# A feed-forward's first rows in their own memory, a shared expert's output by pairs of tiles, and sums spread before a transposition

## The chip, the cores and the metric

The kernel runs on one core of a Trainium2 chip. A core has five engines with their own instruction streams: TensorE (PE in the profile; PEld is its weight load), VectorE (DVE), ScalarE (ACT), GpSimd (POOL) and SyncE (SP). POOL and SP issue most DMAs. The metric is the device time in microseconds (us) of one execution. The kernel before takes 1120.72 us (median of three runs, 1116.92 to 1121.18).

## The reference

x is 4 x 512 rows of 512 numbers, 2048 rows in all, 16 tiles of 128. Four layers follow each other, each on a layer-normalized x, each added to x with a gain:

```
x = x + tanh(g_xattn[0]) * L0_xattn(layernorm(x), itok, ctx)    # 4 gated experts, chosen by token id, weights = ctx
x = x + tanh(g_ffn[0])   * L0_ffn(layernorm(x), wg, wu, wd)     # gated, 512 -> 2048 -> 512, block floating point
x = x + tanh(g_xattn[1]) * L1_xattn(layernorm(x), ctx, ctx)     # softmax attention, 8 heads, times gamma
x = x + tanh(g_ffn[1])   * L1_ffn(layernorm(x), ...)            # 64 experts, 6 per row, plus a shared expert
```

In the feed-forward of layer 0 activations and weights are rounded in blocks of 32 to a shared exponent and a short mantissa. The shared expert of the last layer is

```
shared = silu(x @ ws_gate) * (x @ ws_up) @ ws_down              # 512 -> 192 -> 512
```

## The kernel before

The stages run one after the other and pass x through memory.

**Routed layer (to about 228 us).** Rows are sorted by their token's expert into 19 tiles. The loop `for i in range(-2, NS)` is a software pipeline written out by hand: per step it turns tile i's activations (sT) and tile i+2's rows (hT) with TensorE transposes that ACT copies out of PSUM, multiplies them with the context, squashes and gates, and scatters y_sb with an accumulating indirect DMA (L495, POOL) into `x_rows`. Beside it, `some_weights(us)` hands DVE and ACT a stretch of the rounding of the feed-forward's weights; `turn_weights` transposes what is rounded. A `while` loop behind it finishes the weights. The engines' order here is the order of the program text.

**Feed-forward (to 480).** Every row tile j is loaded from x_rows (`load`, L670, SP), then: sums for the layer norm (`sums_of`: two ACT passes with accumulation, L150), factors for a group of tiles (`factors_from`: a chain of small DVE operations with three Newton steps, L156 to L163), scaling (`normal`, ACT), rounding (`block_scales`, `block_round`, DVE; ACT spreads the scale as mx_wide, L694), transposes (`turned_rows`, h_ps L731, hT L733), gate and up products in four chunks (`gate_up`, L758), silu (ACT) and the product (`times_up`, DVE, L769), rounding of the hidden row, transposes, `down`, and an accumulating store to x_rows. Tile j+1 is prepared inside step j. Nine buffers `xt` hold the rows, in memory that the routed layer used until its end. Here and in the attention PE, ACT and DVE follow the text; SP and POOL are ordered by a scheduler.

**Attention (to about 750).** One loop over n = 4 j + i. Step (j, i) computes the scores of a pair of heads' quarter (at_s, L632), their maxima (low, DVE L637) and exponentials (p, ACT L646), and transposes the p of two steps earlier (p_ps L958, pT L959; two PSUM buffers of tag "t", which h_ps of `turned_row` shares). Beside it goes work for earlier tiles: `values` (at_o, L991), `over_sums` (the reciprocal of the sums, DVE), `spread_sums` (over_ps, L972: 16 small matmuls that lay the reciprocals over the columns; ACT scales them into r, L977), `weighted` (r times at_o, DVE L999), `attended`, `row`, `turned_row` (h_ps L1034, hT L1039), `first_layer` (router and, for the six tiles AT_ONCE, the shared expert's first products, L1048), `hidden_at_once`, `groups_of`, `experts_of` (top-k on DVE) and `noted` (scatters, POOL). over_ps, at_o, at_ps and first_ps share two PSUM buffers of tag "m".

**Experts and shared output (to the end).** For each of 64 experts rows are gathered (POOL), turned, multiplied with weights streamed by SP, and scattered with accumulation, even experts into `out`, odd ones into `more_rows`; the last one goes into `out`. Then, for each of 16 tiles, `turn_shared` transposes the tile's 192 hidden numbers in two halves of 96 (L1441), ACT copies them out, two matmuls of 96 rows with `shared_dn` give sh_y (L1451), DVE adds the tile of `more_rows` (rest, L1453), and POOL issues an accumulating store into `out` (L1454).

## Time and profile before

| what | us |
|---|---|
| median of the runs | 1120.72 |
| the profiled execution | 1129.35 |
| its span | 1127.6 |
| PE busy | 989.6 (88%) |
| DVE busy | 747.5 (66%) |
| ACT busy | 586.6 (52%) |
| POOL busy | 387.6 (34%) |

Rows of the profile read: start, duration, engine, line of the kernel, operation, output<-inputs, shapes, count; in brackets the engine's idle time just before and what ended it. A row of the busy time by stretches gives a stretch, its length, and the busy time of PE, PEld, DVE, ACT and POOL with instruction counts, then the granted TensorE clock, the busy share of the DMA engines and GB/s. PE's starts are recorded, its ends modelled.

### The profile page before, as it was taken

Reading aid. Unit: us, or ns where it says so; the run is one execution under the profiler, and the core shown is the slowest. Engines: PE = TensorE matmul, PEld = TensorE weight load, DVE = VectorE, ACT = ScalarE, POOL = GpSimd, SP = SyncE. Lnnn points to the kernel's source line nnn. Section 1 sums busy time; section 2 is a strip of 40 time slices with the busy share of each in tenths; the row PEclk is TensorE's granted clock in tenths of the full one; section 3 lists DMA queues with packets and bytes.
Section 4 is the critical chain, followed back from the end, with each engine's and each line's share of the span. In section 5 each row is a group of like instructions: output and inputs, shape, how many; then the busy total and the mean of one; then the engine's idle time right before and its main releaser. Section 6 shows DMA issues by size and latency. Waiting matters only on the chain.

```text
span 1127.6 us, 14846 instructions
## 1 busy us (share of the span) xinstructions
PE 989.6 (88%) x4630; PEld 506.9 (45%) x4652; DVE 747.5 (66%) x1877; ACT 586.6 (52%) x1151; POOL 387.6 (34%) x526
## 2 busy tenths in 40 slices
PE   4689999736989898899999989987999999999996
PEld 3345554312444444354454544544444444444442
DVE  6899999958999999848888887864222222222222
ACT  4878886546767668586666766641112111111221
POOL 4123322200000000011554545555455555555434
PEclk9699999857999999999999999997999999999998
DMA  7846655330222121193121221015999999999569
GB/s 255 309 122 142 147 112 141 49 120 27 57 47 38 19 24 24 19 304 110 60 67 50 68 69 41 30 41 190 295 342 325 310 308 303 304 308 316 155 171 162
DMA packets 81438, 168.68 MB, mean 150 GB/s; under 512 B 14637, under 2 KB 15677, under 8 KB 81296
## 3 DMA queue, kind: packets, MB, share of 16 engines
q1 hardware_dynamic: 57440, 128.06, 33.7%
q0 software_dynamic: 23200, 39.08, 18.6%
q8 instruction: 38, 0.62, 0.2%
q10 hardware_dynamic: 720, 0.59, 0.2%
q14 instruction: 40, 0.33, 0.1%
HBM read 133.76 MB, written 44.20 MB: 158 GB/s over the span
## 4 chain that ended last, share of the span: by engine, by line
PE 40%; DVE 9%; ACT 4%; issue 2%; POOL 2%; DMA 0%; POOLq 0%; DVEq 0%; ACTq 0%
PE gu_ps L1335 15%; PE e_y L1357 5%; PE at_o L991 4%; PE e_y L1419 3%; DVE low L637 3%; ACT p L646 2%; PE g_ps L1325 2%; PE first_ps L1048 2%; PE at_s L632 2%; PE at_s L1075 2%; ACT pT L959 1%; PE p_ps L958 1%; POOL out_dram L1454 1%; PE sh_y L1451 1%; PE over_ps L972 1%
## 5 line engine op out<-in xcount | busy, mean ns | idle before, releaser
L1335 PE MATMUL gu_ps<-e_gu,gT 128*96 128x384 f32 x512 | 175.7, 486 | 0.0
L1340 DVE SCALAR_TENSOR_TENSOR a<-s,xg,gu_ps 96x192 f32<-96x192 f32 x64 | 26.2, 409 | 146.5 <-ACT s L1337 146.5
L1337 ACT ACTIVATE s<-gu_ps 96x192 f32<-96x192 f32 x64 | 20.9, 327 | 177.7 <-PE gu_ps L1335 177.6
L123 POOL DMA_INDIRECT taken<-token_no,to_i x96 | 95.6, 996 | 37.8 <-issue 23.9
L646 ACT ACTIVATE p<-at_s,low 128x512 f32<-128x512 f32 x128 | 87.8, 700 | 38.4 <-DVE low L637 22.3
L1335 PEld LDWEIGHTS gu_ps<-e_gu,gT 128*96 128x96 f32 x512 | 78.5, 163 | 61.8 <-issue 61.6
L1311 POOL DMA_INDIRECT xg<-h_rows,idx x64 | 63.7, 996 | 99.4 <-DVE a L1340 67.6
L785 POOL DMA_DIRECT2D x_rows<-y_sb x15 | 12.8, 856 | 239.0 <-ACT y_sb L784 176.1
L637 DVE TENSOR_REDUCE low<-at_s 128x2 f32<-128x1024 f32 x64 | 77.7, 1216 | 17.8 <-PE at_s L632 17.8
L495 POOL DMA_INDIRECT x_rows<-y_sb,to_row x19 | 38.3, 2016 | 142.3 <-ACT y_sb L494 142.3
L758 PEld LDWEIGHTS <-hT 128*128 128x128 bf16 x512 | 51.3, 102 | 72.5 <-issue 19.2
L478 PE MATMUL l_mm<-cT,sT 128*128 x152 | 73.7, 630 | 10.5 <-ACT sT L465 10.5
L959 ACT COPY pT<-p_ps 128x512 f32<-128x512 f32 x128 | 69.4, 604 | 25.2 <-PE p_ps L958 22.7
L478 PE MATMUL l_mm<-cT,hT 128*128 x152 | 71.6, 615 | 9.2 <-ACT hT L465 9.2
L758 PE MATMUL gu<-wgT,hT 128*128 128x512 bf16 x246 | 69.6, 400 | 9.5 <-DVE inter L769 7.0
L958 PEld LDWEIGHTS p_ps<-ident,p 128*128 128x128 f32 x512 | 54.8, 141 | 48.1 <-ACT pT L959 24.7
L632 PE MATMUL at_s<-c_tile,q 64*128 64x512 f32 x256 | 72.0, 640 | 4.9 <-ACT p L646 4.9
L1327 DVE COPY gT<-g_ps 128x384 f32<-128x384 f32 x64 | 35.5, 557 | 61.4 <-PE g_ps L1325 58.9
L776 PE MATMUL y<-wdT,iT 128*128 128x512 bf16 x250 | 61.6, 391 | 11.3 <-ACT iT L751 11.2
L958 PE MATMUL p_ps<-ident,p 128*128 128x128 f32 x512 | 70.2, 280 | 0.4 <-ACT pT L959 0.2
L758 PE MATMUL gu<-wuT,hT 128*128 128x512 bf16 x250 | 67.7, 393 | 0.2
L1357 PE MATMUL e_y<-e_dn,eaT 128*96 128x512 f32 x128 | 65.5, 593 | 0.1
(260 smaller groups left out, 2005.2 us busy)
## 6 DMA issues: line engine op xcount, KB each, us to landing
e_gu<-in_L_ffn_w_gate_dram SPq DMA_DIRECT2D x64, 384.0 KB
e_gu<-in_L_ffn_w_up_dram SPq DMA_DIRECT2D x64, 384.0 KB
e_dn<-in_L_ffn_w_down_dram SPq DMA_DIRECT2D x32, 768.0 KB
w_src<-in_L_ffn_w_gate_dram SPq DMA_DIRECT2D x8, 512.0 KB
c_sb<-in_ctx_dram SPq DMA_DIRECT2D x4, 1024.0 KB
w_src<-in_L_ffn_w_up_dram SPq DMA_DIRECT2D x8, 512.0 KB
more_rows<-zeros SPq DMA_DIRECT2D x16, 256.0 KB
w_src<-in_L_ffn_w_down_dram SPq DMA_DIRECT2D x8, 512.0 KB
```

Source lines behind the costliest of these rows:

```text
L123: ins = nc.gpsimd.indirect_dma_start(out=table[:, :], out_offset=bass.IndirectOffsetOnAxis(ap=to, axis=0), in_=what, in_offset=None)
L478: nc.tensor.matmul(ps.unsqueeze(1), aT[:, k, :], cT[:, bass.ds(at + k, 1), :], start=k == 0, stop=k == KC - 1)
L632: nc.tensor.matmul(s[:, h, :], t["q"][rows, bass.ts(i, P)], t["c"][rows, :], start=True, stop=True)
L637: nc.vector.tensor_reduce(low, tiles[j]["s", i], AX.X, ALU.max, negate=True)
L646: nc.scalar.activation(p[:, h, :], s[:, h, :], AF.Exp, bias=low[:, h : h + 1], accum_out=t["sums"][:, i, h : h + 1])
L758: nc.tensor.matmul(ps[:, i, :], hT[:, k, :], wT[:, k, bass.ts(c, 512)], start=k == 0, stop=k == KC - 1)
L776: nc.tensor.matmul(stages[j]["y"], iT[:, c, :], wdT[:, c, :], start=c == 0, stop=c == FI // P - 1)
L958: nc.tensor.transpose(ps[:, k, :], p[:, h, bass.ts(k, P)], ident)
L959: nc.scalar.copy(tiles[j]["pT"][h][:, :, bass.ts(i, P)], ps)
L1311: gathered_by[e] = nc.gpsimd.indirect_dma_start(out=g[:, :], out_offset=None, in_=h_rows[:, :], in_offset=bass.IndirectOffsetOnAxis(ap=idx ...
L1335: nc.tensor.matmul(ps, gT[:, k, :], gu[:, :, k, :], start=k == 0, stop=k == KC - 1)
L1357: nc.tensor.matmul(y, aT, dn, start=True, stop=False)
```

## The change

Three parts. (1) A pool `ffn_rows` of four buffers is opened before the routed layer, in memory of its own; tiles 0 to 3 (and later 9 to 12) of the feed-forward use it, the others five buffers in the old place. Their loads are issued inside the routed layer, ahead of the `while` loop. One round of `some_weights` moves from the end of step NS-2 to behind the sT transposes of step NS-1. The layer norm of tiles 0 to 3 is taken on DVE (`factors_of`: bn_stats and bn_aggr, tile 0 alone, 1 to 3 together) instead of by ACT's passes, and the order before the feed-forward's loop is rewritten so that tile 1 is normalized and rounded, and tile 2 normalized, there. (2) `shared_dn` is laid out as three blocks of 128 rows, in four DMAs, with 64 rows of it at both halves of the middle block; two tiles' 384 hidden numbers are turned in three transposes; each tile's output is one matmul of 128 rows and one of 64. (3) In the attention `spread_sums` is placed ahead of `turned_row`, and `hidden_at_once` ahead of `groups_of`.

```diff
+    rows_pool = tc.tile_pool(name="ffn_rows", bufs=4, side="right")
+    ffn_rows = rows_pool.__enter__()
+    later_rows = [{} for _ in range(NT)]
+
+    def load(j):
+        pool, n = (ffn_rows, 4) if j % 9 < 4 else (fp, 5)
+        xt = pool.tile([P, D], F32, name="xt", bufs=n)
+        nc.sync.dma_start(xt, x_rows[bass.ts(j, P), :])
+        later_rows[j]["x"] = xt
...
             if i >= 0:
                 turned(i, "s", "sT")
+            if i == NS - 1:
+                some_weights(3.6)
...
-            some_weights(3.6)
+            if i != NS - 2:
+                some_weights(3.6)
             factors_from(i + 4)
+        for j in range(4):
+            load(j)
         while rounded or sources or begun:
...
-        groups = [[0], [1, 2, 3], [4, 5, 6, 7], [8, 9, 10, 11], [12, 13, 14, 15]]
+        groups = [[4, 5, 6, 7], [8, 9, 10, 11], [12, 13, 14, 15]]
...
+        def factors_of(g):
+            mv = few.tile([P, len(g), 2], F32, name="ln_mv", tag=f"ln_mv{len(g)}", bufs=1)
+            for i, j in enumerate(g):
+                st = few.tile([P, 6], F32, name="ln_st", bufs=1)
+                nc.vector.bn_stats(st, stages[j]["x"])
+                nc.vector.bn_aggr(mv[:, i, :], st)
+            a = few.tile([P, len(g)], F32, name="ln_a", tag=f"ln_a{len(g)}")
+            nc.vector.tensor_scalar(a, mv[:, :, 1], EPS, None, ALU.add)
+            y = newton(a, small=few)
+            shift = few.tile([P, len(g)], F32, name="ln_shift", tag=f"ln_shift{len(g)}")
+            nc.vector.scalar_tensor_tensor(shift, mv[:, :, 0], -1.0, y, ALU.mult, ALU.mult)
+            for i, j in enumerate(g):
+                stages[j]["stats"] = y[:, i : i + 1], shift[:, i : i + 1]
...
-        for j in range(8):
+        for j in range(4, 8):
             load(j)
-        sums_of(0)
-        factors_from(0)
+        factors_of([0])
         normal(0)
-        sums_of(1)
         block_scales(0, "h", D)
         block_round(0, "h", D)
-        sums_of(2)
         turned_rows(0)
+        for j in range(4, 7):
+            sums_of(j)
+        factors_of([1, 2, 3])
+        normal(1)
         gate_up(0, 0)
         gate_up(0, 1)
-        sums_of(3)
+        block_scales(1, "h", D)
+        block_round(1, "h", D)
         silu(0, 0)
-        factors_from(1)
         silu(0, 1)
-        normal(1)
-        for j in range(4, 7):
-            sums_of(j)
+        normal(2)
...
-    shared_dn = moe.tile([FH, 2, D], F32, name="shared_dn")
+    shared_dn = moe.tile([P, 3, D], F32, name="shared_dn")
...
-        nc.sync.dma_start(shared_dn, ws_down.rearrange("(c p) d -> p c d", p=FH))
+        FL = P // 2
+        for p, n, c, first in ((0, P, 0, 0), (0, FL, 1, P), (FL, FL, 1, 0), (0, P, 2, FL)):
+            nc.sync.dma_start(shared_dn[bass.ds(p, n), c, :], ws_down[bass.ds(first, n), :])
...
                 do(over_sums, j - 1)
+                do(hidden_at_once, j - 3)
                 do(groups_of, j - 3)
                 do(noted, j - 4, range(3))
-                do(hidden_at_once, j - 3)
...
             elif i == 1:
+                do(spread_sums, j - 1)
                 do(turned_row, j - 2)
-                do(spread_sums, j - 1)
...
-        def turn_shared(j):
-            ps = ps_t.tile([FH, 2, P], F32, name="a_ps", tag="t")
-            for c in range(2):
-                nc.tensor.transpose(ps[:, c, :], shared_a[:, j, bass.ts(c, FH)], ident)
-            aT = xp.tile([FH, 2, P], F32, name="aT")
+        def turn_shared(a):
+            ps = ps_t.tile([P, 3, P], F32, name="a_ps", tag="t")
+            two = shared_a[:, a : a + 2, :].rearrange("p j f -> p (j f)")
+            for c in range(3):
+                nc.tensor.transpose(ps[:, c, :], two[:, bass.ts(c, P)], ident)
+            aT = xp.tile([P, 3, P], F32, name="aT")
             nc.scalar.copy(aT, ps)
             return aT
...
-            for c in range(2):
-                nc.tensor.matmul(y, this[:, c, :], shared_dn[:, c, :], start=c == 0, stop=c == 1)
+            for i, y in enumerate(ys):
+                nc.tensor.matmul(y, this[:, 2 * i, :], shared_dn[:, 2 * i, :], start=True, stop=False)
+            for i, y in enumerate(ys):
+                half = bass.ts(i, P // 2)
+                nc.tensor.matmul(y, this[half, 1, :], shared_dn[half, 1, :], start=False, stop=True)
```

Inside the feed-forward's loop, step 0 no longer normalizes tile 2 or rounds tile 1, as both are done ahead of it.

More of the change, by code (lines that the diff above doesn't have):

```diff
@@ L665, in flamingo_kernel @@
     ):
-        stages = [{} for _ in range(NT)]
-        def load(j):
-            xt = fp.tile([P, D], F32, name="xt", bufs=9)
-            nc.sync.dma_start(xt, x_rows[bass.ts(j, P), :])
-            stages[j]["x"] = xt
+        stages = later_rows
         def part_of(j, what):
@@ L797, in factors_from @@
         def factors_from(j):
-            if j < NT and group_of[j][0] == j:
+            if j in group_of and group_of[j][0] == j:
                 g = group_of[j]
@@ L839, in flamingo_kernel @@
             silu(j, 2)
-            if j + 2 < NT:
+            if 0 < j < NT - 2:
                 normal(j + 2)
@@ L843, in flamingo_kernel @@
                 block_scales(j, ("a", 0), FI // 2)
-            else:
+            elif j:
                 block_scales(j + 1, "h", D)
@@ L850, in flamingo_kernel @@
                 block_round(j, ("a", 0), FI // 2)
-            else:
+            elif j:
                 block_round(j + 1, "h", D)
@@ L906, in flamingo_kernel @@
         add_rows(NT - 1)
+    rows_pool.__exit__(None, None, None)
     mx_pool.__exit__(None, None, None)
@@ L1446, in flamingo_kernel @@
         aT = turn_shared(0)
-        for j in range(NT):
-            y = ps_m.tile([P, D], F32, name="sh_y", tag="m")
-            this, aT = aT, turn_shared(j + 1) if j + 1 < NT else None
-            for c in range(2):
-                nc.tensor.matmul(y, this[:, c, :], shared_dn[:, c, :], start=c == 0, stop=c == 1)
-            o = rest[j // 3][:, j % 3, :]
-            nc.vector.scalar_tensor_tensor(o, y, half_f1, o, ALU.mult, ALU.add)
-            nc.gpsimd.dma_start(out[bass.ts(j, P), :], o, accum_op=ALU.add)
+        for a in range(0, NT, 2):
+            this, aT = aT, turn_shared(a + 2) if a + 2 < NT else None
+            ys = [ps_m.tile([P, D], F32, name="sh_y", tag="m") for _ in range(2)]
+            for i, y in enumerate(ys):
[3 more added lines that the diff above has]
+                nc.tensor.matmul(y, this[half, 1, :], shared_dn[half, 1, :], start=False, stop=True)
+            for i, y in enumerate(ys):
+                j = a + i
+                o = rest[j // 3][:, j % 3, :]
+                nc.vector.scalar_tensor_tensor(o, y, half_f1, o, ALU.mult, ALU.add)
+                nc.gpsimd.dma_start(out[bass.ts(j, P), :], o, accum_op=ALU.add)
 _INS = ['x', 'itok_BxS_13_99985', 'ctx_2048', 'g_xattn', 'g_ffn', 'L0_ffn_w_gate', 'L0_ffn_w_up', 'L0_ffn_w_down',
```

## The prediction

> **What bounds the kernel now.** I read the busy time by stretches first, to see the stages: TensorE is busy 287.5 of 289 us in the experts, 219 of 240 in the attention, but 10.7 of 29 where the feed-forward begins.

> ```profile
> 231.00:260.00 29.00, 10.70 (x41) 4.45 (x40) 12.08 (x47) 17.80 (x40) 0.00 (x0) 0.62 0.32 103
> 260.00:480.00 220.00, 189.88 (x1042) 92.00 (x1060) 204.71 (x325) 151.18 (x227) 12.84 (x15) 0.96 0.19 31
> 510.00:750.00 240.00, 219.47 (x1316) 118.87 (x1316) 195.55 (x747) 159.76 (x388) 117.34 (x270) 0.99 0.18 57
> 796.00:1085.00 289.00, 287.54 (x1122) 137.85 (x1122) 76.93 (x195) 56.15 (x131) 147.75 (x121) 1.00 0.95 287
> ```

> After the length stand the busy us of PE, PEld, DVE, ACT and POOL, the granted clock, DMA share and GB/s. From 260 to 480 DVE is the full engine, so what the head of that stage saves passes on.

> Second, the timelines at that head. DVE rounds weights without a gap until 230.06; nothing ready stands behind it.

> ```profile
> 228.09 0.84 SPq L586 DMA_DIRECT2D c_tile<-in_ctx_dram  x2
> 229.37 0.69 DVE L280 TENSOR_TENSOR w_q<-w_q,mx_wide 128x1024 bf16<-128x1024 bf16 x1
> 231.29 2.70 SPq L670 DMA_DIRECT2D xt<-x_rows  x6
> 234.35 0.72 ACT L150 ACTIVATE waste<-xt 128x512 f32<-128x512 f32 x1 [2.51 <-DMA xt<-x_rows]
> 236.04 0.17 DVE L156 TENSOR_SCALAR ln_mean<-ln_sums 128x2 f32<-128x2 f32 x1 [5.98 <-ACT waste L150]
> 243.36 0.58 PE L731 MATMUL h_ps<-ident_bf,mx_c 128*128 128x128 bf16 x4 [12.20 <-DVE mx_c L716]
> 259.15 0.43 DVE L716 TENSOR_TENSOR mx_c<-mx_c,mx_wide 128x512 bf16<-128x512 bf16 x1 [4.34 <-ACT mx_wide L694]
> 259.63 0.61 PE L731 MATMUL h_ps<-ident_bf,mx_c 128*128 128x128 bf16 x4 [5.03 <-DVE mx_c L716]
> 260.92 1.89 PE L758 MATMUL gu<-wgT,hT 128*128 128x512 bf16 x4 [0.68 <-ACT hT L733]
> ```

> The row loads start when the weights' last reader (PE, 231.16) frees the memory, the sums wait for them, TensorE stands still for 12.2 us, and again for 5.0 us because ACT does six passes of sums (252.39 to 257.33) ahead of tile 1's mx_wide.

> Third, the waits in the attention, then its timelines: thirteen times TensorE waits before h_ps, because h_ps needs the PSUM buffer that ACT's first pT copy frees; over_ps, ready, stands behind it.

> ```profile
> PE h_ps L1034 <- ACT pT L959: 9.3, 13, 1.2
> 643.16 0.66 PE L1034 MATMUL h_ps<-ident,hw 128*128 128x128 f32 x4 [0.81 <-ACT pT L959]
> 643.75 1.09 PE L972 MATMUL over_ps<-ident,over 128*64 128x128 f32 x16
> 644.67 3.60 PE L991 MATMUL at_o<-pT,cT 128*64 128x512 f32 x16
> 650.27 0.69 DVE L999 TENSOR_TENSOR r<-at_o,r 128x512 f32<-128x512 f32 x1 [1.88 <-PE p_ps L958]
> ```

> Last, the end of the run, by stretches: the DMA share, not TensorE, is what stays full.

> ```profile
> 1098.49 0.95 POOL L1454 DMA_DIRECT2D out_dram<-rest  x1 [6.34 <-DMA out_dram<-e_o,idx]
> 1102.00:1104.00 2.00, 2.00 (x8) 0.98 (x7) 0.75 (x1) 0.37 (x1) 2.00 (x5) 1.00 1.01 123
> 1110.00:1112.00 2.00, 2.00 (x7) 0.92 (x6) 0.75 (x1) 0.37 (x1) 0.92 (x2) 1.00 1.12 202
> 1118.00:1120.00 2.00, 0.00 (x0) 0.00 (x0) 0.64 (x1) 0.00 (x0) 0.92 (x2) 1.00 1.13 193
> 1120.00:1122.00 2.00, 0.00 (x0) 0.00 (x0) 0.00 (x0) 0.00 (x0) 0.00 (x0) 0.73 1.11 174
> ```

> **First rows (first part).** The moved round of weights puts ACT's sT copy of the last routed tile (214.42) ahead of one mx_wide and one mx_e (1.03 and 1.04 us); its transposes end at 212.31, so sT starts at about 212.6, the last product, y_sb and the scatter come 1.8 us or more earlier. DVE's order does not change: nothing of DVE's lies between the two places. The scatter landed by 228.09 (the first load that waited for it); now by 226.3. The four new loads need only that landing, as their memory was never used: the first lands 3.06 us after issue (231.29 to 234.35), at 229.3, under DVE's weights, which end at 230.06. On SP they go ahead of two c_tile loads, pushed back by 4 x 0.42 us and needed at 473; no weight load is behind them (the last went at 200.45).

> From 230.1: one bn_stats 0.69, one aggregate 0.18, then 13 small operations at 0.19 to 0.20 (the same count as the row's chain from 236.44 on): 3.4 us, to 233.5. The scaling on ACT starts at 233.6 instead of 239.49. mx_c follows at 237.3 (243.14), the first product at 239.1 (245.02). Three more bn_stats and aggregates and one Newton chain (2.7 + 2.5 us) end on DVE at 242.5, beside ACT's six passes for tiles 4 to 6 (4.94 us, from 238.7 to 243.6); the loads of 4 to 7 go at 231.29 as before and cover that. Then normal(1) 0.8, scales and rounding 2.8: mx_c of tile 1 at 247.2 (before 259.58). Now times_up(0,0) is what is late: it stands behind that rounding on DVE, 247.2 instead of 249.32, so the third and fourth gate products start at 247.9 after 2.7 us of idle TensorE and end near 252.0 (254.6 before). The transposes of tile 1 follow at once, its products start at 253.3 to 253.5 instead of 260.92: **-7.4 us**. If DVE's first small tiles lie in memory that the weights' last reader holds, everything starts at 231.2: -6.3. That is one end; the other is -8.0, if the third and fourth products run at the 1.73 us each that they take from 250.99 on, where I allow 4.1 for both after an idle stretch.

> **Sums' spreading (third part).** over_ps (16 matmuls, 0.92 us from start to start) needs `over`, which DVE has at 641.85; TensorE is free at 642.35. It fills the wait, h_ps (0.59) follows, at_o starts earlier by the idle time. What is added is two more changes between whole-array and 64-column matmuls. Four h_ps took 0.59 to the next start where eight p_ps took 0.93 to 1.03: about 0.12 us for a change. So a tile gains its idle minus 0.12: 0.51 where it was 0.63, 0.68 where 0.80. [...]

> Does the gain reach the end? It does where DVE stood idle before weighted (L999), since DVE there waits for the chain through at_o; tiles whose query factors fall in (528.71, 597.81, 669.69) show no idle before it and give nothing, nor does 509.36, behind a late load. Ten are left: 0.58, 0.58, 0.68, 0.64, 0.51, 0.69, 0.68, 0.68, 0.89, 0.51. Tiles at 579.81 and 616.87 are capped by their DVE idle; the one at 720.35 also saves the 0.38 wait of at_o for shared_a, which hidden_at_once ahead of groups_of removes (two operations, 0.6 us, same DVE sum). **-6.4 us**; ends: 0, and -12.2 (all idle before h_ps, 10.7, plus 1.5 for shared_a). I take the count by tile, which is nearest to rows. ACT now does r before hT; the p_ps that needs hT's buffer is 0.5 us later than the copy.

> **Shared output in pairs (second part).** Loading shared_dn takes four DMAs, 768 KB for 384 KB. At 350 GB/s, the rate from 490 to 510, 393 KB more are 1.1 us, in front of the out store and the x_tile load for which DVE waits 5.32 us at 508.53; three more issues at 0.62 us make 1.9 on SP. **+1.1**, ends 0 and +1.9.

> On TensorE a pair of tiles is 2 x 1.94 = 3.88 us now; after it, two whole products (1.72), a pair of 64-row ones (1.03, the row of e_y L1419) and three transposes (0.33): 3.08, 6.4 us less over eight pairs. But the sixteen accumulating stores may begin only at 1098.49, when the last expert's scatter has landed, and then move 4.2 MB at about 203 GB/s with DMA share 1.1 until 1123. At 1106 ten were issued and about four moved; the queue never runs dry, so an earlier issue only lengthens it. **0 us**; ends: -5.8 if issue set the end (last issue 1118.93 to 1113.1), +1.3 if the slow first rate (143 KB/us while POOL issues back to back) lasts for all 14 us of issuing.

> **Sum.** -7.4 - 6.4 + 1.1 + 0 = -12.7 us. The experts in between keep TensorE full, and their weights, landed by 1054 for a last use at 1079, shift with it. Against the profiled execution (1129.35, span 1127.6) that is 1116.6. It was 8.6 us slower than the median of the runs, 1120.72; from the median: **1108.0**.

> **Rivals.** (A) The swap gives nothing: the added changes of matmul shape eat it, or weighted waits for something else. For it: five times DVE waited for ACT's r, not for at_o. Then -6.3 in all: 1114.4. (B) The head moves less, about 3 us: the scaled tile or its scratch waits for freed memory, or ACT's six passes still delay tile 1. Against it: DVE ended at 230.06 with idle to 236. Then 1112.4. (C) The tail follows TensorE after all: 5.8 more, 1102.2; against it the share of 1.1. (D) Slower: r, now ahead of hT on ACT, comes late. Seven r waited up to 2.04 us after hT though over_ps was long done (544.84 against 539.67). hT then ends about 2.1 us after p_ps wants its buffer and TensorE stalls. On all 13 tiles, 2.1 each and no gain, it is 27.3 - 7.4 + 1.1: +21, 1141.7. It decides from 0.92 us lost per tile, (5.6 + 7.4 - 1.1) / 13. Against it: eight r waited not at all, and h_ps now stands between over_ps and at_o. (E) The change does not do what it says: the first rows still land after 231, head -2, others as forecast: 1113.4.

> **How the numbers follow.** Differences under 0.5% (5.6 us) can't be told from none here. Forecast, 1104 to 1112: 0.48. A 0.17, B 0.10, C 0.08, D 0.09, E 0.08. Faster: the forecast, B, C, E (0.74) and, since A lies at -6.3, just past the bound, a third of it: 0.80; same: the rest of A, 0.11; slower: D, 0.09. The range leaves out D and the outer edge of C and A: 1101 to 1117, with the tail's ends and the shared_dn load inside it.

> **What would show it.** Right: xt loads issued before 228 and landed by 230; bn_stats at 230 to 231.3; tile 1's products near 253.4; no wait of h_ps for pT, over_ps in front of it; r's waits no longer; sh_y in steps of about 3.1 us a pair, the DMA share still 1.1 to the end and 23 to 25 us from the first accumulating store to the last byte. Wrong: hT's copy late and p_ps waiting for it; DVE's first bn_stats after 232; a tail shorter by over 2 us.

## The result, and the profile after

The changed kernel takes 1110.02 us (median of seven runs, 1107.29 to 1112.90) against 1120.72 us for the kernel before (median of seven runs, 1116.26 to 1121.32). The ratio is 0.9916, with a 95% interval of 0.9896 to 0.9935: 9.4 us less, between 7.3 and 11.7 (the ratio's distance from 1 times 1120.72). The forecast was 1108.0 and 1101 to 1117. The profiled execution took 1109.52 us (span 1107.7), so unlike the profile of before it lies at its median.

The two profiles are not in step where the change begins: the last gated product of the routed layer starts on DVE at 209.74 before and at 207.69 after. Times below that are called aligned have these 2.05 us added. First the stretches of the changed kernel, as busy us of PE, PEld, DVE, ACT and POOL, granted clock, DMA share and GB/s:

```profile
225.00:254.00 29.00, 14.56 (x63) 6.62 (x64) 19.95 (x58) 14.86 (x31) 0.00 (x0) 0.68 0.31 99
254.00:470.00 216.00, 187.95 (x1053) 91.00 (x1053) 202.71 (x323) 148.69 (x222) 12.85 (x15) 0.97 0.19 31
490.00:730.00 240.00, 230.46 (x1371) 124.98 (x1371) 200.26 (x751) 166.27 (x407) 118.45 (x277) 0.97 0.22 73
776.00:1065.00 289.00, 288.69 (x1125) 138.24 (x1126) 76.05 (x194) 56.28 (x129) 148.81 (x121) 1.00 0.96 287
```

TensorE is busier at the head of the feed-forward (14.6 of 29 us, 10.7 before) and in the attention (230 of 240, 219 before); the experts are as they were. The granted clock in the attention is 0.97 where it was 0.99: this small figure becomes the main finding below.

The head, from the timelines of SP's queue, ACT, POOL, DVE and PE:

```profile
210.48 0.58 ACT L476 COPY sT<-l_ps 128x512 f32<-128x512 f32 x1
221.35 2.06 SPq L191 DMA_DIRECT2D xt<-x_rows  x4
223.98 0.69 DVE L821 BATCH_NORM_STATS2 ln_st<-xt 128x6 f32<-128x512 f32 x1 [2.09 <-DMA xt<-x_rows]
229.61 0.69 DVE L291 TENSOR_TENSOR w_q<-w_q,mx_wide 128x1024 bf16<-128x1024 bf16 x1
231.96 0.82 ACT L170 ACTIVATE h<-xt,ln_shift,ln_y 128x512 f32<-128x512 f32 x1
237.11 1.89 PE L770 MATMUL gu<-wgT,hT 128*128 128x512 bf16 x4 [0.68 <-ACT hT L745]
246.21 1.25 PE L770 MATMUL gu<-wgT,hT 128*128 128x512 bf16 x4 [4.04 <-DVE inter L781]
252.68 1.04 PE L770 MATMUL gu<-wgT,hT 128*128 128x512 bf16 x4 [0.94 <-ACT hT L745]
```

The loads go out at 221.35 and the first row has landed by 223.98. DVE takes its statistics not behind the weights, as the order of the program text would have it, but in the middle of them, so DVE does not keep to the text there, and waits 2.09 us; the weights then end at 230.30. The second tile's products start at 252.68, aligned 254.73, where they started at 260.92: 6.2 us.

One ordinary tile of the attention, on PE and DVE:

```profile
626.30 1.09 PE L999 MATMUL over_ps<-ident,over 128*64 128x128 f32 x16
627.32 0.66 PE L1061 MATMUL h_ps<-ident,hw 128*128 128x128 f32 x4
627.91 3.65 PE L1018 MATMUL at_o<-pT,cT 128*64 128x512 f32 x16
632.10 0.67 DVE L1026 TENSOR_TENSOR r<-at_o,r 128x512 f32<-128x512 f32 x1
```

No bracket is left: over_ps fills what h_ps waited for, and r no longer waits (1.88 us in the line shown of before). An ordinary tile takes 14.7 us from r to r where it took 16.7.

The end of the run, POOL's timeline and one stretch:

```profile
1078.59 0.95 POOL L1491 DMA_DIRECT2D out_dram<-rest  x1 [7.30 <-DMA out_dram<-e_o,idx]
1094.27 0.85 POOL L1491 DMA_DIRECT2D out_dram<-rest  x1 [0.42 <-issue]
1097.00:1099.00 2.00, 0.00 (x0) 0.00 (x0) 0.00 (x0) 0.00 (x0) 0.00 (x0) 0.50 1.14 206
```

From the first accumulating store to the end of the span there are 29.1 us, as before (1098.49 to 1127.56), though the last store is issued 15.7 us behind the first instead of 20.4.

By the traces alone the attention would have won 11.4 us (243.3 from the first r to the fifteenth before, 231.9 after) and the head 6.2, some 7 us more than the times show (9.4 by the ratio, 10.7 by the medians). The experiments had to find which of the two sides misleads.

### The profile page after: what moved, and what is told of

The parts are those of the page before. It is cut to its first block, busy times and chain, and to the rows that moved or that the text cites. A ratio compares the mean times of both kernels' runs of the same rounds, so it can differ in the third digit from the quotient of the medians.

```text
span 1107.7 us, 14785 instructions
## 1 busy us (share of the span) xinstructions
PE 985.5 (89%) x4644; PEld 503.5 (45%) x4644; DVE 749.2 (68%) x1879; ACT 577.0 (52%) x1127; POOL 384.5 (35%) x526
## 4 chain that ended last, share of the span: by engine, by line
PE 46%; DVE 8%; ACT 1%; issue 1%; DVEq 0%; POOLq 0%; POOL 0%
PE gu_ps L1365 15%; PE e_y L1387 5%; PE at_s L649 4%; PE p_ps L985 3%; PE at_o L1018 3%; PE e_y L1449 3%; PE first_ps L1075 2%; PE g_ps L1355 2%; PE at_s L1102 2%; DVE low L654 2%; PE sh_y L1483 1%; PE over_ps L999 1%; PE sh_y L1486 1%; PE ea_ps L1380 1%; ACT p L663 1%
## 5 line engine op out<-in xcount | busy, mean ns | idle before, releaser
L770 PE MATMUL gu<-wgT,hT 128*128 128x512 bf16 x256 | 69.6, 397 | 14.6 <-DVE inter L781 13.0
L788 PE MATMUL y<-wdT,iT 128*128 128x512 bf16 x256 | 62.8, 391 | 10.7 <-ACT iT L763 10.7
```

The lines of the kernel that those rows point to most:

```text
L770: nc.tensor.matmul(ps[:, i, :], hT[:, k, :], wT[:, k, bass.ts(c, 512)], start=k == 0, stop=k == KC - 1)
L788: nc.tensor.matmul(stages[j]["y"], iT[:, c, :], wdT[:, c, :], start=c == 0, stop=c == FI // P - 1)
```

## The parts alone

Each of the first three kernels is the kernel before with one part of the change; the fourth exchanges two lines only:

```
 # swap_only
             elif i == 1:
+                do(spread_sums, j - 1)
                 do(turned_row, j - 2)
-                do(spread_sums, j - 1)
 # attn_only: the same, and hidden_at_once ahead of groups_of (i == 0)
 # rows_only: ffn_rows, load, the moved some_weights(3.6), factors_of, the new order of tiles 0 to 2
 # pairs_only: shared_dn in four transfers, turn_shared(a) and the loop over pairs
```

> The kernel before with the first part alone (first rows in memory of their own, the moved round of weights, the new order of the first tiles). By the forecast's first term it is 7.4 us faster than the kernel before. By the trace of the changed kernel, where the first row's bn_stats stands in the middle of the weights and waits 2.09 us there, it is about 6.2 us. In the profile the second tile's first gate product starts 6 to 7.4 us earlier against the last routed tile's gated product on DVE. Rival: the head is worth 3 us or less, because the feed-forward's later tiles, which DVE bounds, take the rest back.

> The kernel before with the second part alone (shared_dn loaded in four transfers, shared output in pairs of tiles). By the forecast: slower by 1.1 us (0 to 1.9), the end of the run unchanged, 29.1 us from the first accumulating store to the end of the span. Rival: since the profile shows 16 us less between the two kernels than the medians do, less the lateness of the profiled execution, this part may cost 4 to 6 us that the trace of the changed kernel does not show: then this kernel is 4 to 6 us slower.

> The kernel before with the third part alone (sums' spreading ahead of the second row's turning, and the hidden products one step earlier). By the forecast: 6.4 us faster, 0.5 to 0.7 us per ordinary tile, only the idle time before h_ps. Rival, from the trace of the changed kernel: 11 us faster, 0.75 per tile on the average and 1.5 to 2 per ordinary tile, because r (L999) also stops waiting 1.9 us past the end of at_o. If the trace shows 11 and the time 6 or less, the extra was the profiled execution's own.

> The kernel before with one pair of lines exchanged: sums' spreading ahead of the second row's turning; the hidden products stay in their old place. By the forecast: 5.9 us faster, that is the third part without the 0.5 us of the tile at 720.35 that hidden_at_once frees. Rival: the gain hangs on both lines together (shared_a earlier on DVE is what shortens r's wait); then this kernel is less than 3 us faster.

Measured on one chip, called the first below, beside 1120.28 us for the kernel before (35 runs):

| kernel | median, us | ratio, 95% interval | us from the ratio |
|---|---|---|---|
| rows_only | 1113.19 | 0.9945, 0.9921 to 0.9968 | -6.2 (-8.8 to -3.6) |
| pairs_only | 1120.78 | 1.0005, 0.9983 to 1.0027 | +0.6 (-1.9 to +3.0) |
| attn_only | 1116.78 | 0.9969, 0.9951 to 0.9988 | -3.5 (-5.5 to -1.3) |
| swap_only | 1116.10 | 0.9958, 0.9938 to 0.9977 | -4.7 (-6.9 to -2.6) |

The three parts add up to -9.1, the whole is -9.4: within intervals of two to three us each, nothing shows that they hinder each other. The head is worth what the trace of the changed kernel says. The pairs are worth nothing that can be told from none. The attention is worth 3.5, half the forecast and a third of what the two first traces show.

The trace of pairs_only, whose attention has the order of before, says why the first traces mislead. One of its tiles, DVE and PE:

```profile
689.13 3.60 PE L991 MATMUL at_o<-pT,cT 128*64 128x512 f32 x16
692.85 0.69 DVE L999 TENSOR_TENSOR r<-at_o,r 128x512 f32<-128x512 f32 x1 [0.93 <-PE at_o L991]
```

r starts 0.12 us behind the end of at_o (689.13 + 3.60), where the profile of before showed 2.0 (644.67 + 3.60 to 650.27). From the first r to the fifteenth this kernel takes 234.1 us, rows_only 234.9; the profile of before, with the same order, 243.3. So 8.4 to 9.2 us of the apparent gain belong to that one profiled execution, which was 8.6 us above its median: its lateness lay in the attention. Beside 234.1 the changed kernel's 231.9 is a gain of 2.2.

## Where the rest of the swap's gain went

In the changed kernel two steps from r to r are longer than in pairs_only, though its ordinary steps are shorter: 18.14 for 16.80 at the seventh, 16.45 for 14.78 at the eleventh. Both follow a tile in which DVE works out the query factors. PE's timeline there, and the stretches around it:

```profile
653.35 1.97 PE L1075 MATMUL first_ps<-first_w,hT 128*128 128x64 f32 x8 [2.27 <-DVE r L1026]
655.25 2.08 PE L649 MATMUL at_s<-c_tile,q 64*128 64x512 f32 x4
650.00:653.00 3.00, 1.08 (x11) 0.94 (x9) 2.55 (x15) 0.28 (x1) 0.00 (x0) 1.00 0.26 98
654.00:657.00 3.00, 3.00 (x11) 1.64 (x10) 2.36 (x7) 2.02 (x7) 0.30 (x2) 0.50 0.23 87
657.00:660.00 3.00, 3.00 (x12) 2.07 (x12) 2.27 (x7) 1.32 (x3) 1.98 (x11) 0.52 0.29 87
```

TensorE stands idle for 2.27 us, because first_ps needs the PSUM buffer that r frees, and r stands behind the query factors on DVE. Then the granted clock is 0.50 for 6.8 us, and four score products take 2.08 us for 1.13. In the old order the same gap is 1.01 us (pairs_only) and the clock stays at 1.00. The swap lets TensorE be done earlier; here, where DVE sets the pace, the gap grew from 1.01 to 2.27 us, and the clock fell to 0.50.

The next kernels give TensorE other work in that gap: at the three tiles, first_layer stands behind the next scores.

```
-            elif i == 3:
+            elif i == 3 and j not in (3, 7, 11):
                 do(squashed, j - 2)
 
             if n >= 2:
                 scores(j, i)
+                if i == 3 and j in (3, 7, 11):
+                    do(first_layer, j - 2)
+                    do(squashed, j - 2)
                 highest(j, i)
...
                 do(attended, j - 1)
-                do(first_layer, j - 2)
+                if j not in (3, 7, 11):
+                    do(first_layer, j - 2)
```

gap_filled is the changed kernel with this edit, gap_filled_before the kernel before with it. hidden_only is the kernel before with `do(hidden_at_once, j - 3)` ahead of `do(groups_of, j - 3)`; before_again is the kernel before as it is.

> The changed kernel with one thing more: at the three tiles of the attention where DVE computes the query factors (j = 3, 7, 11), first_layer stands behind the next scores instead of ahead of them, so that the two score products fill the time in which TensorE waits for DVE. In the changed kernel TensorE stands idle there for 2.04, 2.36 and 2.27 us, and its granted clock then falls to 0.50 for 3 to 6.5 us. Theory (the swap makes these gaps longer, and the clock that they cost takes back half of the swap's gain): the gaps fall to about 1 us, the granted clock between 480 and 735 us stays at 1.00, and the time falls by 3 to 4 us against the changed kernel, to about 1106 to 1107. Rival (the clock at these places costs nothing, since DVE sets the pace there): the same time as the changed kernel, 1109.5 to 1110.5.

> The same move of first_layer in the kernel before. There the gaps are 1.24, 1.50 and 1.01 us and the clock fell behind two of the nine that the profiles of this order show. Theory: little to win, 0 to 1.5 us. Rival (the move is good in itself, clock or not): the same 3 to 4 us as in the changed kernel.

> The kernel before with hidden_at_once one place earlier, ahead of groups_of, and nothing else. By the forecast: 0.4 to 0.5 us faster at the most, the wait of at_o for shared_a. By the theory of the gaps: that wait (0.37 to 0.39 us) is taken from a place ahead of a DVE-bound gap, so that 0 is won. Rival: since the third part won less than the exchange of lines alone (3.5 against 4.7 us), this line costs about 1 us.

> The kernel before, unchanged, for a second profile. If the profiled execution that the forecast was read from was late in the attention alone, the way from the first r (L999) to the fifteenth, 243.3 us there, is 234 to 235 us here, as in the two kernels that keep its order of the attention; r then waits at most 0.3 us in the first half. Rival: 243 us again, and the order is slower with the other two parts as they were.

These four ran on another chip, where the kernel before takes 1124.67 us (23 runs). gap_filled: ratio 0.9928 (0.9911 to 0.9946), 8.1 us less. gap_filled_before: 0.9989 (0.9974 to 1.0005), 1.2 us less, not to be told from none. hidden_only: 0.9990 (0.9978 to 1.0001), 1.1 less, not to be told from none either. before_again: 1124.8.

The clock behaved as expected, it is 1.00 throughout the attention in gap_filled, but its ratio is no better than the 0.9916 of the changed kernel, and before_again missed its expectation. Its PE and DVE, once more at_o and r:

```profile
690.94 3.60 PE L991 MATMUL at_o<-pT,cT 128*64 128x512 f32 x16
696.43 0.69 DVE L999 TENSOR_TENSOR r<-at_o,r 128x512 f32<-128x512 f32 x1 [2.58 <-PE p_ps L958]
```

r is 1.89 us late, and 239.2 us pass from the first r to the fifteenth. All four profiles of this chip show r late, from the fourth at_o on, by 1.1 to 2.6 us at most of the tiles where DVE waits for it (in gap_filled, where over_ps does not stand directly ahead of at_o, too); the eight profiles of the first chip show 0.1 to 0.4 at such tiles, and 0.8 at one where ACT's r is the later one. So in these twelve profiles it goes with the chip, not with the program; the profile of before shows the late kind, the profile after the prompt kind, and on which chips these two were taken is not on record. Where r is late, TensorE waits for it at most tiles (from 530 us on nine times in gap_filled), not at the three alone, and the changed kernel itself did not run on that chip: gap_filled alone can't judge the theory.

So the changed kernel and gap_filled ran side by side on the first chip (after_again, gap_filled_2), with hidden_back, the changed kernel with `do(hidden_at_once, j - 3)` in its old place behind noted, and half_the_stores, which leaves out the accumulating stores of the odd tiles:

```
-                nc.gpsimd.dma_start(out[bass.ts(j, P), :], o, accum_op=ALU.add)
+                if i == 0:
+                    nc.gpsimd.dma_start(out[bass.ts(j, P), :], o, accum_op=ALU.add)
```

> The changed kernel, unchanged, beside the next two on one chip. Expected: 0.990 to 0.993 of the kernel before, as the first result. If r (L1026) comes 2 us behind the end of at_o here, as in the profile of the kernel before, the way from the first r to the fifteenth is about 237 us; if it comes within 0.2 us, 232 us.

> first_layer behind the next scores at the three tiles with the query factors, now beside the changed kernel. Theory (the three falls of the clock cost the changed kernel about 3.7 us: 0.3, 1.5 and 1.9 from its steps beside those of the kernels without a fall): 3 to 4 us faster than the changed kernel, at a granted clock that is 0.005 higher, where r follows at_o at once. Where r comes 2 us late, TensorE waits for r at every tile and the gaps are no longer the bound: then 1 us or less. Rival: no gain in either case.

> The changed kernel with hidden_at_once back behind noted, as before the change; the exchange of sums' spreading and second row's turning stays. By the forecast: 0.4 to 0.5 us slower, the wait of at_o for shared_a. By the theory of the gaps: at_o then waits about 1.05 us for shared_a at the tiles that are turned at once, which shortens the third gap from 2.3 to 1.0 us and keeps the clock there; 0 to 1.5 us faster than the changed kernel.

> The changed kernel with the accumulating stores of the odd tiles left out (eight of sixteen; their rows lack this last sum). By the forecast (the end is set by the bytes of these stores, 4.2 MB at about 203 GB/s): from the first of them to the end of the span 18 to 20 us instead of 29.1, the time 9 to 11 us shorter. Rival (the end follows TensorE, whose last product ends 13 us after the first store): the end falls by 0 to 2 us.

r is prompt here again (the kernel before: 1121.05 us, 11 runs).

| kernel | median, us | ratio to before, 95% interval | first r to fifteenth, us | granted clock, 480 to 735 |
|---|---|---|---|---|
| after_again | 1109.92 (1109.82 to 1110.63) | 0.9905, 0.9881 to 0.9928 | 232.0 | 0.97 |
| gap_filled_2 | 1104.33 (1099.60 to 1106.52) | 0.9850, 0.9823 to 0.9878 | 225.9 | 1.00 |
| hidden_back | 1108.22 (1106.21 to 1113.73) | 0.9898, 0.9870 to 0.9926 | 231.2 | 0.99 |
| half_the_stores | 1103.75 (two runs) | 0.9848, 0.9811 to 0.9886 | 232.3 | 0.97 |

The place of the third gap in gap_filled_2, PE's timeline and the stretches:

```profile
647.57 1.13 PE L649 MATMUL at_s<-c_tile,q 64*128 64x512 f32 x4
649.92 1.10 PE L1075 MATMUL first_ps<-first_w,hT 128*128 128x64 f32 x8 [1.22 <-DVE r L1026]
650.00:653.00 3.00, 2.38 (x18) 1.97 (x20) 2.83 (x7) 3.00 (x10) 0.00 (x0) 1.00 0.38 139
653.00:656.00 3.00, 1.92 (x14) 1.09 (x12) 2.76 (x9) 2.29 (x7) 1.99 (x11) 1.00 0.05 18
```

The scores fill the time, the gap is 1.22 us and the clock stays at 1.00. The kernel is 5.6 us faster than the changed one (1104.33 for 1109.92; the slowest of its six runs, 1106.52, is below the fastest of the other's, 1109.82), more than the 3 to 4 expected, and 6.1 us of it are found between the first r and the fifteenth: 2.74 at the seventh step (18.28 to 15.54), 2.18 at the eleventh (16.52 to 14.34). The rival, that these places cost nothing since DVE sets the pace there, is out. But gap_filled_2 removes idle time and the falls together, so by itself it doesn't say which of them cost the time. That the same edit gave the kernel before only 1.2 us (-0.6 to 2.9) speaks for the clock rather than the new order, with the reserve that this was on the chip of the late kind.

hidden_back tells the two apart. It has one gap of 2.04 us left and one fall; the other two gaps are 1.24 and 1.02, since at_o now waits for shared_a ahead of them (0.74 and 1.05 us). At the third gap, PE's timeline and the stretch behind it:

```profile
644.13 3.65 PE L1018 MATMUL at_o<-pT,cT 128*64 128x512 f32 x16 [1.05 <-DVE shared_a L1092]
651.27 1.10 PE L1075 MATMUL first_ps<-first_w,hT 128*128 128x64 f32 x8 [1.02 <-DVE r L1026]
653.00:656.00 3.00, 3.00 (x21) 1.71 (x18) 2.83 (x9) 2.40 (x8) 1.05 (x6) 1.00 0.53 175
```

TensorE has the same work in the same order as in after_again and stands idle nearly as long (1.05 + 1.02 us, there 2.27 in one piece), but its clock stays at 1.00. From first_ps to the next over_ps it takes 7.94 us (651.27 to 659.21) instead of 10.40 (654.26 to 664.66), and the eleventh step is 14.34 us instead of 16.52, the same 2.18 as in gap_filled_2. So the clock, not the idle time, is what costs there: TensorE at half clock is late for the tile behind. At the seventh step, where hidden_back keeps the gap and the fall, nothing is won (18.46 for 18.28). The order of before has a second case: the first gap is 1.24 us in rows_only and in pairs_only, the clock fell behind it in rows_only alone, and the step behind it is 15.38 us there for 14.86.

At the other tiles the wait for shared_a costs about what the clock gives back: hidden_back is 0.8 us faster by the ratios, which can't be told from no difference. The forecast had this line as a gain of 0.4 to 0.5.

half_the_stores lasts 21.2 us from the first store to the end of the span (1080.89 to 1102.1) instead of 29.1, and is 6.2 us faster than the changed kernel. Its last store, POOL's timeline:

```profile
1094.89 0.84 POOL L1492 DMA_DIRECT2D out_dram<-rest  x1 [2.12 <-DVE rest L1490]
```

It is issued 14.0 us behind the first, nearly as late as with all stores (15.7), and POOL now waits for the sums. So the bytes do set the end in the changed kernel, but half of them take only 8 us off, since the pace of the products is next in line: the expected 9 to 11 us were too many, the rival's 0 to 2 too few.

## Why the prediction was right, point by point

The time came 2.0 us above the forecast (1110.02 for 1108.0), well inside the range. The sum was -12.7; the ratio says -9.4 (-11.7 to -7.3), the medians -10.7. Two terms were too large and the errors add.

**First rows: -7.4 forecast, -6.2 measured** (rows_only, and the trace after, aligned). The steps hold one by one, in aligned times: scaling 234.0 for 233.6, mx_c 237.3 for 237.3, first product 239.2 for 239.1, third gate product 248.3 for 247.9. The loads went out at 223.4, ahead of the 226.3 that the forecast had. That DVE runs the chain behind its weights, "From 230.1", was wrong: it moved in among the weights, which then end at 232.35, but the chain had to be run anyway, and 0.4 was lost at the scaling and nothing at mx_c. What was mis-sized is the last step, "I allow 4.1 for both after an idle stretch": the third and fourth products took 5.1 us in the changed kernel (246.21 to 251.35), 3.4 of them at half clock (246.87 to 250.29). In rows_only they did not, with the idle time 3.41 instead of 4.04 us:

```profile
248.48 1.02 PE L770 MATMUL gu<-wgT,hT 128*128 128x512 bf16 x4 [3.41 <-DVE inter L781]
253.26 1.04 PE L770 MATMUL gu<-wgT,hT 128*128 128x512 bf16 x4 [0.94 <-ACT hT L745]
```

There four products take 1.03 each, and from the gated product (209.70) to the second tile's products it is 43.6 us, against 51.2 before and 45.0 after: 7.6 less, the forecast's far end of -8.0 nearly. So this last step hangs on whether the clock has come back. The runs of rows_only (-8.8 to -3.6) can't tell 6.2 from 7.6, so that its median agrees with the changed kernel's trace to a tenth is chance.

**Sums' spreading: -6.4 forecast, -3.5 measured (-5.5 to -1.3).** The mechanism held: over_ps stands in the wait, h_ps no longer waits for pT (but 1.17 us once at the end, where it was 1.16 before), at_o starts earlier, the added change between whole-array and 64-column matmuls costs little (over_ps and h_ps take 1.61 us to the start of at_o, 626.30 to 627.91, for 1.51 before, 643.16 to 644.67), and hT's later copy stalls p_ps no more than before, 0.19 us once at the end in both. The size failed in two places. "Ten are left", the count by tile, was read from an execution in which r was 2 us late; in the prompt kind DVE waits for r a quarter of a microsecond or nothing in the first half. And the tiles with query factors, which "show no idle before it and give nothing", gave less than nothing: TensorE's gap ahead of first_ps grew to 2.0 to 2.4 us and the clock fell. With the gaps filled the part is worth 8.2 us between the first r and the fifteenth (234.1 in pairs_only, 225.9 in gap_filled_2); the longer gaps and their falls take back 6.1. The forecast's value lay between the two for a reason that it did not have: that it came out within 3 us is luck. The term's end of 0 would need changes of matmul shape that cost all of the idle time ahead of h_ps, 0.63 to 0.81 us at most tiles; no run shows that, the rows just named differ by 0.10 us.

**Shared output in pairs: +1.1 forecast, +0.6 measured (-1.9 to +3.0).** In the traces it is 0: the steps at the late load are 15.01 and 20.02 us with the longer shared_dn load (pairs_only) and 15.02 and 20.04 without it (rows_only). The 5.32 us that DVE waited for x_tile in the profile of before are not the rule: it is 4.28 both in pairs_only and in rows_only, so the longer load delays nothing there.

**Tail 0: right.** 29.1 us before, after and in pairs_only alone (29.0), with the last issue 4.7 us earlier; rival C is out. The DMA share falls to 0.02 from 1103 on, 24.4 us behind the first store, where the forecast's sign was 23 to 25. A pair's products took 3.25 us (1072.62 to 1075.87) for the forecast's 3.08, which cost nothing. half_the_stores puts what half the bytes would win at 6 to 8 us.

Rivals A and B are out by the parts' own times, E by the loads that had landed at 223.98, and D, which decided from 0.92 us lost per tile, by p_ps, which waits for hT once, 0.19 us, as before. But D had the right kind of thought, that what is moved can make something else late: it looked at ACT, and it was the clock.

## What to carry to other kernels

Before counting on a gain tile by tile, see that the profile's own time is near the median, and get a second profile where it is not: here 8.6 us of 1129 sat in just the stage that the change touched. Where TensorE, made faster, then waits for a slower engine, look at the granted clock behind the gap: behind gaps of 2.0 to 2.4 us its next products ran at half clock here, and moving ready work into them (four score products ahead of first_layer at three tiles) was worth 5.6 us, where the exchange of lines itself was worth 4.7. The best kernel of this study is the changed one with that move, 0.985 of the kernel before.

## What the runs showed of the hardware that was not expected

**Short gaps and the clock.** In the fourteen profiles there are 14 gaps of 2.01 to 2.36 us ahead of first_ps at the three tiles, and the granted clock fell to 0.50 behind all 14; of 25 gaps between 0.98 and 1.73 us it fell behind 3. A fall lasts 3.4 or 6.8 us: in the changed kernel the clock is 0.50 from 519.94 to 523.35, from 584.79 to 588.21 and from 653.06 to 659.89.

The length of a gap doesn't decide alone. In the feed-forward (262 to 470 us) the same profiles have 49 gaps of 3.22 to 3.38 us, and behind 15 of them the clock did not fall. One of these, in pairs_only:

```profile
384.18 0.40 PE L731 MATMUL h_ps<-ident_bf,mx_c 128*128 128x128 bf16 x4 [3.23 <-DVE mx_c L716]
379.01:382.42 3.41, 1.89 (x14) 1.01 (x13) 3.01 (x16) 0.84 (x2) 0.00 (x0) 1.00 0.64 77
382.42:385.84 3.42, 1.66 (x11) 0.92 (x12) 3.23 (x6) 3.06 (x5) 0.00 (x0) 1.00 0.00 0
385.84:389.25 3.41, 3.41 (x18) 1.54 (x16) 3.31 (x4) 1.62 (x2) 0.00 (x0) 1.00 0.02 5
```

**r late by chip.** On one chip DVE starts r mostly 0.12 us behind the end of at_o, on another mostly 1.1 to 2.6 us behind it, with the same order of instructions; the first at_o, 0.11, is prompt on both, the fourth is the first that shows the lag. It is issued in the step in which POOL's indirect stores of token numbers (`noted`) begin. Whether these have to do with it was not tried; the cause stays open. Each table and each group of runs above compares kernels on one chip.
